# A sparse-graph network: the second layer's product 2 takes two of eight column blocks over edge lists, and list 0 is made in layer 0

## The chip, the cores and the metric

The kernel runs on one core of one Trainium2 chip. The core has a matrix engine (TensorE, PE in the profile), VectorE (DVE), ScalarE (ACT), GpSimd (POOL), and SyncE (SP), whose queue issues most loads; sixteen DMA engines are shared by all queues. Each engine works through its own instructions in the order that was fixed when the program was built. The metric is the device time of one execution in microseconds, smaller is better: the median of the runs.

## The reference

There are N = 4096 nodes with 128 features. The adjacency matrix `adj` is 4096 x 4096 in float32: about 0.2% of the entries are nonzero in symmetric places (each with a value of its own, from 0.05 to 1), and so is the diagonal. Four layers follow each other, each added to its input and normalized:

```
layer 0:  hw = x W;  e = leaky_relu of sums of hw over neighbours
          x <- norm(x + (softmax of e over a row's neighbours, times adj) hw)
layer 1:  twice cheb_conv(h) = h W[0] + (adj h) W[1] + (2 adj (adj h) - h) W[2] + b, then elu
layer 2:  attention of 4 heads over the columns of adj
layer 3:  x Ws + (adj x / row degree) Wn
```

The case is about layer 1 (the "second layer"). Its first convolution needs t1 = adj x (product 1) and adj t1 (product 2, for t2 = 2 adj t1 - x). The second one is arranged so that it takes two more products, of v (product 3) and of w (product 4).

## The kernel before

**Dense products.** `propagate` (L683) forms a product transposed, one block of 512 output columns at a time: for each of eight blocks `ib` it goes through eight chunks `c` of `adjT` (128 partitions x 4 x 512 floats, 1 MB each, loaded by SP's queue into a pool `ld` of five buffers, L661), with four matmuls of 128 x 512 each (L691), which the profile counts as two records each. So a product is 8 x 8 chunks. After each chunk a callback `seen(ib, n, c, a)` may add other work; a call of it is called a hook here. A block of `adj` columns is named by its number, 0 to 7; four tiles of 128 nodes make one.

**Edge lists.** Once the nonzeros of a block of four tiles are known, its product can be done by gathering the neighbours' rows instead: six near entries and three shared slots per node (`NEAR`, `QT`). The steps are
- `take` (L1319): for chunk (`ib`, `c`), the eight largest entries of each of four tiles' rows and their places, two VectorE instructions a tile (L1331, L1332). The list of block c needs all eight chunks (ib, c). On the diagonal chunk a copy by ACT (L1326) and three VectorE instructions (L1328 to L1330) take the own entry out and keep it in `diag`.
- `build` (L1340): three parts, each a `next`, that sort these into indices; small matmuls (L1382, L1406) stand between the parts.
- `pairs` (L1461) or `values` (L1455): gathers on Pool that fetch the entries' values, one indirect DMA for every 128 of them (L1452), each followed by a tiny "pause" (L1498). `pairs` gets both directions' values for the blocks in `PAIRED`; there are 4 x 9 gathers a block. `paired` (L1468) copies them to where they are used, in program order.
- `rows_of` (L1477): nine gathers that fetch one tile's neighbour rows from a table in DRAM, written by `store` (L1493) from ACT's queue. `weigh` (L1482): ACT scales the own row, three VectorE instructions make the slots' weights (L1486), and six add the near rows (L1489). Then PE multiplies, three or four matmuls of 128 x 128.

**Where they are used before the change.** Takes of even blocks run beside product 1, of odd blocks beside product 2. Beside product 2 the lists of blocks 0, 2 and 4 (`PAIRED`) are built and their 108 pairs gathered. Product 3 (`third_product`, L1528) does five blocks densely, and the twelve tiles of `PAIRED` over lists, beside building the other five lists. Product 4 (in `sparse_layers`, L1590) does six densely and the eight tiles of `LAST` = 0, 2 over lists. Layers 2 and 3 use all lists.

**Layer 0** (L281) works on the same chunks, row block by row block. For each chunk VectorE makes a mask (`masks`, L326), PE takes sums over the mask (L385), ACT looks for negative entries (L369), and PE multiplies (L397). From row block 2 on PE's order is written out by hand (`in_order`, L375): a group of mask sums, then that group's products. In block i >= 3 the first group is a chunk that was left over from the block before, then chunks 0 and 1, then another left-over one; then come product 0 and the scores of block i-1 (L427).

**Order.** Outside of parts that are written by hand, a planner orders each engine's instructions: program order decides among those that its model takes to be ready. `keep_in_program_order` pins an instruction behind the one traced before it on its engine.

**End of a block of product 2** (L740 to L754): VectorE makes t2T from the sum (L741), PE multiplies it and others by the first layer's weights (six matmuls of 128 x 512, L745), elu gives `hT`, and eight matmuls of 128 x 128 (L750) give v.

## Time and profile before

| | us |
|---|---|
| median of 3 runs | 1681.68 (1681.07 to 1682.41) |
| the profiled execution's own time | 1683.87 |
| its span (first to last instruction) | 1681.9 |
| layer 0, to the first matmul of product 1 | 0 to 329.8 |
| product 1 | 329.8 to 556.2 |
| product 2 | 556.2 to 846.9 |
| product 3 | 846.9 to 1048.7 |
| product 4, then layers 2 and 3 | 1048.7 to 1681.9 |

| engine | busy us | share of the span |
|---|---|---|
| PE | 1517.7 | 90% |
| DVE | 1089.2 | 65% |
| POOL | 749.3 | 45% |
| ACT | 372.4 | 22% |

A line of instructions gives the start, the length, the engine, the line of the kernel, the operation, the tiles written and read, and a count when several follow each other; in square brackets stands how long the engine stood idle before it and what ended that. A line of waits gives who waited for whom, then the sum, the times and the longest. Busy time is an average: what a change in one stage is worth is read from that stage.

### The profile page before, as it was taken

The numbers are of one execution on the slowest core, as the hardware profiler recorded it, in microseconds if no ns is written. First come the engines' busy times: TensorE is split into PE (matmuls) and PEld (weight loads), VectorE is DVE, ScalarE is ACT, GpSimd is POOL, SyncE is SP. The second block draws the span as 40 slices with busy tenths as digits, with TensorE's granted clock in tenths as the row PEclk, the third lists the DMA queues.
The fourth block names the chain that finished last, engine by engine and source line by source line (L and its number), as shares of the span: only waits on it lengthen the run. The fifth ranks groups of instructions, "written<-read, shape, count | busy, mean of one in ns | idle before, by whom it ended". The sixth has DMA issues, their size and how long they took to land.

```text
span 1681.9 us, 16311 instructions
## 1 busy us (share of the span) xinstructions
PE 1517.7 (90%) x4808; PEld 732.3 (44%) x4808; DVE 1089.2 (65%) x3189; ACT 372.4 (22%) x682; POOL 749.3 (45%) x1180
## 2 busy tenths in 40 slices
PE   6999999999999999999989899999955788889886
PEld 3344344544444444444434445454422344444444
DVE  5664546798779896888659832255434755557676
ACT  4865520100000011011110000022223111112234
POOL 0000000000000045555458888888827888888851
PEclk9999999999999999999989999999976888889988
DMA  9988756578888866777758868988846667778774
GB/s 383 355 314 304 254 200 225 194 288 311 299 298 298 311 209 218 255 247 243 258 203 280 311 224 286 336 296 283 296 108 182 212 199 232 238 235 277 240 198 105
DMA packets 102601, 429.24 MB, mean 255 GB/s; under 512 B 20387, under 2 KB 38822, under 8 KB 60646
## 3 DMA queue, kind: packets, MB, share of 16 engines
q1 hardware_dynamic: 62288, 376.79, 62.8%
q0 software_dynamic: 20352, 31.44, 7.4%
q10 hardware_dynamic: 19862, 19.86, 4.1%
q8 instruction: 40, 0.66, 0.2%
q14 instruction: 59, 0.48, 0.1%
HBM read 416.43 MB, written 11.60 MB: 254 GB/s over the span
## 4 chain that ended last, share of the span: by engine, by line
PE 59%; DVE 16%; DMA 9%; POOL 7%; issue 5%; ACT 2%; ACTq 0%; DVEq 0%; POOLq 0%; SPq 0%
PE pacc L691 24%; PE pacc L397 12%; PE pp L1918 8%; POOL got L1688 6%; DMA got<-table,source 4%; PE pp L1799 3%; DMA chunk<-in_adjT 3%; DVE at L1332 2%; DVE top L1331 2%; DVE gw L1724 1%; PE pden L385 1%; DMA got<-rows,source 1%; PE ptr L340 1%; DVE acc L1812 1%; DVE here L1726 1%
## 5 line engine op out<-in xcount | busy, mean ns | idle before, releaser
L1688 POOL DMA_INDIRECT got<-table,source x288 | 276.0, 958 | 88.6 <-issue 61.4
L1799 PE MATMUL pp<-chunk,xT 128*128 128x512 f32 x496 | 243.9, 633 | 1.2 <-ACT xT L1770 0.7
L691 PE MATMUL pacc<-chunk,t 128*128 128x512 f32 x512 | 223.8, 593 | 0.0
L691 PE MATMUL pacc<-chunk,x 128*128 128x512 f32 x512 | 222.0, 592 | 0.0
L1452 POOL DMA_INDIRECT got<-rows,source x180 | 180.9, 1005 | 60.2 <-issue 50.2
L397 PE MATMUL pacc<-chunk,hw 128*128 128x512 f32 x408 | 188.1, 605 | 1.5 <-DVE numT L425 1.2
L1331 DVE MAX8 top<-chunk 128x8 f32<-128x512 f32 x224 | 144.4, 677 | 55.4 <-DMA chunk<-in_adjT 55.4
L1918 PE MATMUL pp<-chunk,w 128*128 128x512 f32 x384 | 170.2, 592 | 0.0
L1498 POOL TENSOR_TENSOR idle<-v,idle 128x1 f32<-128x1 f32 x7 | 1.5, 211 | 336.5 <-ACT v L752 336.5
L1298 POOL IOTA i<- 128x384 int32 (+3 forms) x4 | 1.0, 260 | 337.1 <-PE pden L385 323.9
L1332 DVE FIND_INDEX8 at<-top,chunk 128x8 uint16<-128x512 f32 x224 | 151.1, 683 | 0.0
L691 PEld LDWEIGHTS pacc<-chunk,x 128*128 128x128 f32 x512 | 96.3, 190 | 116.2 <-issue 116.2
L691 PE MATMUL pacc<-chunk,v 128*128 128x512 f32 x320 | 145.3, 605 | 0.0
L691 PEld LDWEIGHTS pacc<-chunk,t 128*128 128x128 f32 x512 | 95.7, 190 | 113.4 <-issue 113.4
L1799 PEld LDWEIGHTS pp<-chunk,xT 128*128 128x128 f32 x496 | 94.3, 203 | 91.2 <-issue 84.6
L1452 POOL DMA_INDIRECT both_ways<-in_pairs,both_at x108 | 108.0, 1000 | 22.4 <-issue 17.8
L397 PEld LDWEIGHTS pacc<-chunk,hw 128*128 128x128 f32 x408 | 74.7, 191 | 92.7 <-issue 86.7
L328 DVE TENSOR_SCALAR pos<-chunk 128x2048 bf16<-128x2048 f32 x66 | 80.2, 1221 | 42.3 <-DMA chunk<-in_adjT 34.2
L1918 PEld LDWEIGHTS pp<-chunk,w 128*128 128x128 f32 x384 | 70.5, 190 | 76.5 <-issue 76.5
L369 ACT ACTIVATE junk<-chunk 128x2048 fp8e4<-128x2048 f32 x51 | 97.4, 1910 | 26.3 <-DMA chunk<-in_adjT 25.7
L1489 DVE SCALAR_TENSOR_TENSOR here<-got,back,here 128x128 f32<-128x128 f32 x120 | 42.0, 350 | 89.3 <-DMA got<-rows,source 86.3
L1498 POOL TENSOR_TENSOR idle<-idle 128x1 f32<-128x1 f32 x417 | 96.0, 230 | 7.4
(355 smaller groups left out, 1932.2 us busy)
## 6 DMA issues: line engine op xcount, KB each, us to landing
chunk<-in_adjT SPq DMA_DIRECT2D x342, 1024.0 KB, 5.3
keep<-in_adjT SPq DMA_DIRECT2D x13, 1024.0 KB, 10.6
spread<-spread ACTq DMA_DIRECT2D x16, 384.0 KB, 4.5
got<-table,source POOLq DMA_INDIRECT x288
chunk<-in_adjT ACTq DMA_DIRECT2D x4, 1024.0 KB
got<-rows,source POOLq DMA_INDIRECT x180
table<-rows ACTq DMA_DIRECT2D x8, 264.0 KB, 3.9
xT<-in_xT ACTq DMA_DIRECT2D x8, 256.0 KB, 6.6
```

What stands on the lines that cost most here:

```text
L328: r = nc.vector.tensor_scalar(pos, a, 0.0, None, op0=ALU.is_gt)
L369: nc.scalar.activation(junk, a, AF.Relu, scale=-1.0, accum_out=bad[:, n:n + 1], saturate=False)
L397: in_order(nc.tensor.matmul(p, hw[:, j * TB + k, :], a[:, k, :], start=first and k == 0, stop=last and k == TB - 1))
L691: nc.tensor.matmul(p, stationary(c * TB + k), a[:, k, :], start=n == 0 and k == 0, stop=n == NB - 1 and k == TB - 1)
L1331: nc.vector.max(self.top[:, t, ib, :], row)
L1332: nc.vector.max_index(self.at[:, t, ib, :], self.top[:, t, ib, :], row)
L1452: tc.keep_in_program_order(nc.gpsimd.indirect_dma_start(out, None, of, bass.IndirectOffsetOnAxis(ap=index, axis=0)))
L1489: r = nc.vector.scalar_tensor_tensor(here, got[:, j, 0:F], self.back[:, u, j:j + 1], here, op0=ALU.mult, op1=ALU.add)
L1498: return nc.gpsimd.tensor_tensor(self.idle[:, 0:1], of, self.idle[:, 1:2], ALU.mult)
L1688: nc.gpsimd.indirect_dma_start(got[t][:, j, :], None, table, bass.IndirectOffsetOnAxis(ap=lists.source[:, t, j:j + 1], axis=0))
L1799: nc.tensor.matmul(p, y[:, t0 + k, :], a[:, ib % (TB // n), k, :], start=k == 0, stop=k == n - 1)
L1918: nc.tensor.matmul(p, w[:, c * TB + k, :], a[:, k, :], start=n == 0 and k == 0, stop=n == NB - 1 and k == TB - 1)
```

## The change

`PAIRED` becomes 0, 1, 2 and `LAST` 0, 1. In product 2 only blocks 2 to 7 are dense; blocks 0 and 1 go over lists. For that

- the takes of column block 0 move into layer 0 (`first_list`), to the chunk j = 0 of each row block. The host lays the diagonal of `adj` out as an input, so that one instruction takes it off in place of three;
- product 1 takes its blocks in the order 2, 3, 0, 4, 5, 1, 6, 7, with takes of columns 1 to 3, and of 4 to 7 in blocks 0 and 1. List 0 is built beside its second and third block, its 36 pairs are gathered beside the later ones, and t1 is stored as a third table of rows;
- product 2 takes columns 4 to 7 of its six blocks, pinned, and a written plan (`second_product`) says at which of its 48 hooks lists 1 and 2 are built, pairs and rows gathered, and the eight tiles weighed and multiplied. Rows are gathered into parts of `hT`, `t1T` and `xT` that aren't used yet or any more. The end of a block is now a function, called for the list blocks too;
- product 3 builds lists 3 to 7, and its plan is one hook later.

The diff, without its unchanged lines ("..." stands for them):

```diff
-PAIRED = [0, 2, 4]
-LAST = [0, 2]
+PAIRED = [0, 1, 2]
+LAST = [0, 1]
+FAR = [4, 5, 6, 7]
...
-def adj_resnorm_d4(ctx: ExitStack, tc: tile.TileContext, x_in, xT_in, adj, adjT, pairs, w0g, w0gT, a0, w1a, b1a,
+def adj_resnorm_d4(ctx: ExitStack, tc: tile.TileContext, x_in, xT_in, adj, adjT, pairs, diag_in, w0g, w0gT, a0, w1a, b1a,
...
+            def first_list(i, a):
+                top, at = firsts
+                for k in range(TB):
+                    row = a[:, k, :]
+                    if i == 0:
+                        row = x[:, k * TB:(k + 1) * TB, :].rearrange("p t f -> p (t f)")
+                        nc.scalar.copy(row, a[:, k, :])
+                        d = row[:, k * P:(k + 1) * P]
+                        nc.vector.scalar_tensor_tensor(d, ident, less_own[0][:, k:k + 1], d, op0=ALU.mult, op1=ALU.add)
+                    nc.vector.max(top[:, k, i, :], row)
+                    nc.vector.max_index(at[:, k, i, :], top[:, k, i, :], row)
...
+                    if j == 0:
+                        first_list(i, a)
...
+                if j == 0:
+                    first_list(i, a)
...
-    degrees = []
+    degrees, firsts, less_own = [], [], []
...
-                    degrees[:] = [enter(name="degrees", bufs=1).tile([P, NT], F32, name="rowdeg")]
+                    early = enter(name="early", bufs=1)
+                    degrees[:] = [early.tile([P, NT], F32, name="rowdeg")]
+                    firsts[:] = early.tile([P, TB, NB, 8], F32, name="top0"), early.tile([P, TB, NB, 8], U16, name="at0")
+                    own_entries = early.tile([P, NT], F32, name="diag")
+                    less_own[:] = [early.tile([P, NT], F32, name="less_own")]
+                    nc.scalar.dma_start(own_entries, diag_in)
+                    nc.vector.tensor_scalar_mul(less_own[0], own_entries, -1.0)
...
-                    lists = Lists(whole, first, l1h_pool)
+                    lists = Lists(whole, first, l1h_pool, own_entries)
...
-                for ib, blk, p in propagate(lambda jt: x[:, jt, :], finished, seen=lambda ib, n, c, a: c % 2 or lists.take(ib, c, a)):
+                pairs = {c: lists.pairs(c) for c in PAIRED} if usual else {}
+                def fetch(c, n):
+                    for _ in range(n):
+                        next(pairs[c], None)
+                made = lists.build(0) if usual else None
+                done = []
+                def beside_first(ib, n, c, a):
+                    if 0 < c < FAR[0] or ib in LAST and c in FAR:
+                        lists.take(ib, c, a)
+                    if (len(done), n) in ((1, 0), (1, 4), (2, 0)):
+                        next(made)
+                    if len(done) > 2 and n == 3:
+                        tc.keep_in_program_order(lists.pause(t1[:, done[-1] * TB, 0:1]))
+                        fetch(0, TB * 9 // 4)
+                for ib, blk, p in propagate(lambda jt: x[:, jt, :], finished, seen=beside_first, blocks=[2, 3, 0, 4, 5, 1, 6, 7]):
...
+                    done.append(ib)
+                    if usual:
+                        lists.store(2, ib, t1)
...
-                steps, pairs = {}, deque()
-                def fetch(n):
-                    while pairs and n:
-                        if next(pairs[0], pairs) is pairs:
-                            pairs.popleft()
-                        else:
-                            n -= 1
-                for n, c in enumerate(PAIRED if usual else ()):
-                    made = lists.build(c)
-                    steps[2 * n, 0], steps[2 * n, 4] = [lambda made=made: next(made)], [lambda made=made: next(made)]
-                    steps[2 * n + 1, 0] = [lambda made=made: next(made), lambda c=c: pairs.append(lists.pairs(c))]
-                def second(ib, n, c, a):
-                    if c % 2:
-                        lists.take(ib, c, a)
-                    for f in steps.pop((ib, n), ()):
-                        f()
-                    if usual and ib and n == 3:
-                        tc.keep_in_program_order(lists.pause(v[:, ib * TB - 1, 0:1]))
-                        fetch(16)
-                for ib, blk, p in propagate(lambda jt: t1[:, jt, :], seen=lambda ib, n, c, a: second(ib, n, c, a)):
-                    t2T = l1w.tile([P, IB], F32, name="t2T")
-                    nc.vector.scalar_tensor_tensor(t2T, p, 2.0, xT[:, blk], op0=ALU.mult, op1=ALU.subtract)
+                def t2_of(t2T, p, cols):
+                    nc.vector.scalar_tensor_tensor(t2T, p, 2.0, xT[:, cols], op0=ALU.mult, op1=ALU.subtract)
+                def second_end(ib, t2T):
+                    blk = slice(ib * IB, (ib + 1) * IB)
...
+                    done[-1] = ib
...
+                second = second_product(lists, l1w, pairs, t1, t1T, xT, hT, v, done, t2_of, second_end) if usual else None
+                for ib, blk, p in propagate(lambda jt: t1[:, jt, :], seen=second, blocks=[b for b in range(NB) if not usual or b not in LAST]):
+                    t2T = l1w.tile([P, IB], F32, name="t2T")
+                    t2_of(t2T, p, blk)
+                    second_end(ib, t2T)
...
-                    fetch(len(pairs) * TB * 9)
-                    for c in PAIRED:
-                        lists.paired(c)
+                    fetch(PAIRED[-1], TB * 9)
+                    lists.paired(PAIRED[-1])
...
-        def __init__(self, whole, first, layer):
+        def __init__(self, whole, first, layer, own_entries):
...
-            self.tables = [dram.tile([N + 1, F], F32, name=f"rows{n}") for n in range(2)]
+            self.tables = [dram.tile([N + 1, F], F32, name=f"rows{n}") for n in range(3)]
...
-            self.at = keep.tile([P, NT, NB, 8], U16, name="at")
-            self.diag = keep.tile([P, NT], F32, name="diag")
+            self.at = keep.tile([P, NT - TB, NB, 8], U16, name="at")
+            self.diag = own_entries
...
-        def take(self, ib, c, a):
+        def take(self, ib, c, a, pinned=False):
+            pin = tc.keep_in_program_order if pinned else lambda r: r
...
-                    own = self.keep.tile([P, P], F32, name="diagonal")
...
-                    nc.vector.tensor_mul(own, d, ident)
-                    nc.vector.tensor_reduce(self.diag[:, t:t + 1], own, AX.X, ALU.add)
-                    nc.vector.tensor_sub(d, d, own)
-                nc.vector.max(self.top[:, t, ib, :], row)
-                nc.vector.max_index(self.at[:, t, ib, :], self.top[:, t, ib, :], row)
+                    pin(nc.vector.scalar_tensor_tensor(d, ident, less_own[0][:, t:t + 1], d, op0=ALU.mult, op1=ALU.add))
+                pin(nc.vector.max(self.top[:, t, ib, :], row))
+                pin(nc.vector.max_index(self.at[:, t - TB, ib, :], self.top[:, t, ib, :], row))
...
-            top = self.top[:, ts]
+            top, found_at = (self.top[:, ts], self.at[:, (c - 1) * TB:c * TB]) if c else firsts
...
-            nc.vector.tensor_copy(flat(key), flat(self.at[:, ts]))
+            nc.vector.tensor_copy(flat(key), flat(found_at))
...
+    def second_product(lists, pool, pairs, t1, t1T, xT, hT, v, done, t2_of, second_end):
+        units = len(LAST) * TB
+        E = NEAR + QT
+        late = slice(5 * IB, 8 * IB)
+        soon = slice(2 * IB, 5 * IB)
+        places = [t[:, cols].rearrange("p (j f) -> p j f", f=F)
+                  for t, cols in ((hT[:, 0], late), (hT[:, 1], late), (t1T, soon), (xT, soon))]
+        got = places[0:2] + places[2:4] * (units // 2 - 1)
+        made, sums = {}, {}
+        plan = {}
+        def at(h, f, *args):
+            plan.setdefault(h, []).append(lambda: f(*args))
+        def fetch(c, n):
+            for _ in range(n):
+                next(pairs[c], None)
+        def pull(u):
+            deque(lists.rows_of(u, got[u], 2), 0)
+        def weigh(u):
+            here = pool.tile([P, F], F32, name="here2", bufs=1)
+            lists.weigh(u, t1[:, tile_of(u), :], got[u], here, got[u][:, E:E + QT, :], True)
+            made[u] = here
+        def product(u):
+            t, k = tile_of(u), u % TB
+            if k == 0:
+                sums[0] = pool.tile([P, IB], F32, name="t2T")
+            p = lists.psum.tile([P, P], F32, name="u")
+            nc.tensor.matmul(p, made.pop(u), ident, start=True, stop=False)
+            for j in range(QT):
+                nc.tensor.matmul(p, got[u][:, j, :], got[u][:, E + j, :], start=False, stop=j == QT - 1)
+            t2_of(sums[0][:, k * P:(k + 1) * P], p, slice(t * P, (t + 1) * P))
+            if k == TB - 1:
+                second_end(PAIRED[u // TB], sums.pop(0))
+        for c, h in ((1, 0), (2, 8)):
+            build = lists.build(c)
+            for n in range(3):
+                at(h + 3 * n, next, build)
+        at(6, fetch, 1, TB * E)
+        at(11, pull, 0)
+        at(12, pull, 1)
+        at(17, fetch, 2, 9)
+        at(18, lists.paired, 0)
+        at(30, lists.paired, 1)
+        for u, h in enumerate((20, 24, 28, 32, 33, 37, 40, 41)):
+            at(h, weigh, u)
+            at(h + 1, product, u)
+        for u, h in ((2, 25), (3, 25), (4, 29), (5, 33), (6, 34), (7, 38)):
+            at(h, pull, u)
+        at(40, fetch, 2, TB * E)
+        hooks = [0]
+        def seen(ib, n, c, a):
+            h = hooks[0]
+            hooks[0] += 1
+            if c in FAR:
+                lists.take(ib, c, a, True)
+            for f in plan.pop(h, ()):
+                f()
+            if h == 47:
+                assert not plan and not made and not sums
+        return seen
...
-            for c in (6, 1, 3, 5, 7):
+            for c in (3, 4, 5, 6, 7):
...
-        plan = {5: [lambda: deque(lists.values(6), 0)]}
-        for u, h in enumerate((6, 8, 14, 17, 19, 22, 24, 27, 30, 32, 35, 37)):
+        plan = {5: [lambda: deque(lists.values(3), 0)]}
+        for u, h in enumerate((7, 9, 15, 18, 20, 23, 25, 28, 31, 33, 36, 38)):
...
-        plan[36].append(lambda: deque(lists.values(1), 0))
+        plan[36].append(lambda: deque(lists.values(4), 0))
...
-                for c in (3, 5, 7):
+                for c in (5, 6, 7):
...
-            order = [0, 1, 2, 3, 5, 6, 4, 7]
+            order = [0, 1, 3, 4, 5, 6, 2, 7]
...
+        "diag": column_blocks(np.diagonal(adj)),
```

## The prediction

> **What bounds the kernel now.** I read the chain of waits first, then busy time stage by stage, then single instructions. Of the chain that ended last, these lines carry it:
>
> ```profile
> PE 59%; DVE 16%; DMA 9%; POOL 7%; issue 5%; ACT 2%; ACTq 0%; DVEq 0%; POOLq 0%; SPq 0%
> ```
>
> TensorE's matmuls are most of it. Cut into stages (columns: stretch, its length, then busy us and instructions of each engine, granted clock, DMA share, GB/s): layer 0's DMA-heavy start, the rest of layer 0, product 1, product 2, product 3.
>
> ```profile
> 0.00:81.50 81.50, 64.27 (x315) 29.30 (x316) 48.38 (x114) 51.86 (x56) 0.69 (x6) 0.94 0.94 374
> 81.50:329.80 248.30, 245.69 (x927) 110.90 (x926) 140.24 (x333) 95.15 (x114) 0.81 (x5) 1.00 0.70 251
> 329.80:556.20 226.40, 225.79 (x566) 101.81 (x565) 196.20 (x545) 16.13 (x28) 0.59 (x3) 1.00 0.82 295
> 556.20:846.90 290.70, 278.39 (x764) 127.77 (x763) 230.50 (x687) 43.43 (x73) 133.44 (x223) 1.00 0.72 247
> ```
>
> From 81.5 us through product 2 PE is busy nearly all the time; VectorE (third busy figure) is at 57%, 87% and 79% of the last three stretches, and Pool only works in product 2. So a matmul removed from product 2 is time removed, unless VectorE or Pool is made late. Product 2 takes 290.7/8 = 36.3 us per column block. The prices, from the timelines of PE, VectorE and Pool (start, length, what):
>
> ```profile
> 816.34 25.06 PE L691 MATMUL pacc<-chunk,t 128*128 128x512 f32 x58
> ...
> 1079.57 0.39 PE L1894 MATMUL pp<-ident,here 128*128 128x128 f32 x2
> 1079.79 0.83 PE L1896 MATMUL pp<-into,got 128*128 128x128 f32 x6
> 1080.46 3.60 PE L1918 MATMUL pp<-chunk,w 128*128 128x512 f32 x8
> ```
>
> ```profile
> 601.64 1.27 DVE L1331 MAX8 top<-chunk 128x8 f32<-128x512 f32 x2
> ...
> 604.15 0.27 DVE L1354 TENSOR_SCALAR there<-top 128x256 f32<-128x256 f32 x1
> ```
>
> ```profile
> 601.99 1.17 POOL L1452 DMA_INDIRECT both_ways<-in_pairs,both_at  x1 [4.05 <-DVE both_at L1434]
> 603.20 0.20 POOL L1498 TENSOR_TENSOR idle<-idle 128x1 f32<-128x1 f32 x1
> 603.55 0.99 POOL L1452 DMA_INDIRECT both_ways<-in_pairs,both_at  x1 [0.15 <-issue]
> 604.55 0.21 POOL L1498 TENSOR_TENSOR idle<-idle 128x1 f32<-128x1 f32 x1
> 604.92 0.97 POOL L1452 DMA_INDIRECT both_ways<-in_pairs,both_at  x1 [0.15 <-issue]
> ```
>
> 58 of a block's 64 records run from 816.34 to 841.24 (start of the next), 0.43 us each: a dense block is 27.5 us, a chunk 3.44 us. One tile's product over lists is 1080.46 - 1079.57 = 0.89 us. Two tiles of a take (maxima and their places) last from 601.64 to 604.15, so a chunk of four is 5.02 us. Gathers follow each other every 604.92 - 603.55 = 1.37 us (1.36 further on).
>
> Last, where a late gather hits PE today, at the start of product 3:
>
> ```profile
> 868.73 0.35 DVE L1489 SCALAR_TENSOR_TENSOR here<-got,back,here 128x128 f32<-128x128 f32 x1 [7.54 <-DMA got<-rows,source]
> ...
> 876.40 0.16 PE L1382 MATMUL u<-count,below 128*128 128x4 bf16 x1 [8.02 <-DVE count L1358]
> 876.43 6.74 PE L691 MATMUL pacc<-chunk,v 128*128 128x512 f32 x8
> ```
>
> The row read at 868.73 was asked for by the fourth gather, which left Pool at 864.13: 4.6 us to land. VectorE stood at it, the counts behind it came late, PE waited 8.02 us, and its next eight records took 6.74 us instead of the 3.60 of line L1918 above.
>
> **What the Trainium skill says.** Perfetto Trace Analysis, Sequencer Loop: an engine instruction goes into the engine's queue and waits there for its semaphores. The trace agrees: one late row held all of VectorE for 7.54 us. DMA: Bandwidth & Descriptors, Anatomy of one DMA (SWDGE path): about 2.0 us fixed cost, mostly the receipt of the write; the trace shows 4.6 us beside the chunk loads, and I use that. TensorE: Matmul & The Clock Gate, HAM oscillation: PE gaps over about 3.4 us drop its clock; the 6.74 us above agree, so a long stall costs some 3.1 us on top.
>
> **The change part by part.** The sums are against the profiled execution: span 1681.9 us, its own time 1683.9, median of the runs 1681.7; a difference carries over to the median.
>
> *Removed:* two dense blocks of product 2, 2 x 27.5 = 55.0 us of PE, and 16 chunk loads with them (no price: DMA is at 0.72). *Added on PE:* eight products of 0.89 = 7.1 us. The two blocks' ends (hidden layer, v) stay. With nothing late: -47.9.
>
> *Moved: takes of column block 0 into layer 0.* Eight chunks x 5.02 = 40.2, and four diagonal fixes of 0.35 (as L1489, same operands' size): 41.6 us of VectorE, in bursts of 5.0 right behind a chunk's mask and ahead of the next chunk's mask and of the scores. PE there must have the masks in order, and today waits only 4.0 us for them. Block by block: in the start, VectorE has some 7.5 us idle between 38 and 58 us, and gets 6.4 + 5.0 = 11.4: about 4 late, and 1 more with what scores waits for. Block 2's masks are back to back from 68 to 75 and PE wants the last at 76.6: 3.5 late. Block 3: last mask at 107.4, PE at 108.9, 2 us of idle before: 1.8 late. Block 4: the chunks land at 127.5, 130.5 and 134.8, gaps that hold the burst: 0. Block 5: they land 2.5 us apart, burst 2.5 late. Blocks 6 and 7: landings 4 to 6.9 apart: 0. Sum 12.8, less something for the waits it overlaps (1.15 us at 171.4 is one): I take 12. Bounds: 0 (idle takes all) to 41.6.
>
> *Product 1.* Takes are 24 chunks plus 8 extra ones of blocks 0 and 1: 32 as before. But those blocks have seven takes, 35.1 us of VectorE in 28.3 of PE, and list 0 is built around block 0 (some 15 us by its rows from 604 to 608 and 575 to 601). Cover: the takes may lead PE by about 8 us (five chunk buffers, 5.3 us landing) and lag it by 8. Nothing taken; 0 to 6 us if that cover is short. The three-instruction diagonal becomes one: VectorE slack only. The 36 pair gathers run on an idle Pool; eight t1 stores on ACT's queue (256 KB; a like one lands in 3.9 us) are wanted 60 us later; 16 KB of diagonal at the start: nothing.
>
> *Product 2's timing.* Places count from its start. List 1's third part is issued at hook 6, PE 7 x 3.44 = 24.1 us; in the old trace 8.8 us passed from that matmul (593.2) to the first gather (602.0), so Pool starts at 32.9. It has 36 pairs and 9 rows ahead of the first weigh: 45 x 1.36 = 61.2, plus 4.6 landing: 98.7. That weigh is at hook 20, its product behind chunk 21: 2 x 36.3 + 6 x 3.44 = 93.2. PE waits 5.5. Queued on VectorE behind it are three pinned takes, 15.1 us, until 114, and then that block's t2T; PE gets there at 98.7 + 0.9 + 6.9 + 1.7 = 108.2 and waits about 6 more. With 3.1 of lost clock: 14.6. The next rows: tile 2's places are free after block 4 (about 116), Pool idle then; rows at 133 against hook 28 at about 134. Later ones have 5 us or more to spare. Pool ends its 144 gathers at about 249 of some 258, so product 3's start keeps its own stall. I take 15; bounds 0 (VectorE's order lets block 4's end pass) to 25 (the first take of the block is stuck behind the rows too, another 5, and a second tile waits once).
>
> *Product 3 and 4:* five lists to build, 12 and 8 tiles, the same gathers; each weigh one hook later, other column numbers. Zero, give or take 5.
>
> Sum: -47.9 + 12 + 15 = -20.9: 1681.7 - 20.9 = 1660.8, say 1661.
>
> **The rivals.** *Covered everywhere* (chance 0.25): VectorE's 43% idle in layer 0 takes the bursts and the order on VectorE is one that the late row does not block; -47.9 plus 3 to 5: 1637. For it: idle share; against: the masks' leads of 1 to 4 us against bursts of 5. *Gathers slower* (0.13): beside full DMA the pace is nearer 1.5 us (product 3's lines show 1.35 to 2.0). Then the first rows are 45 x 0.14 = 6 later, and a second tile waits, some 5: 1672. Pool is then nearly the bound of the stage: 144 x 1.5 + 33 = 249 plus landing. *Slower than before* (0.12): layer 0's bursts are on PE's path in full. Place: masks and scores of each row block; price 41.6; with the 15 of product 2 that is -47.9 + 56.6 = +8.7, 1690. It decides from 32.9 of the 41.6 on. Against: three blocks have landing gaps that hold a burst. That the change doesn't act, the dense blocks being skipped by name, can't be; the general path would only follow a failed list check, and would take many times the difference. About even (1678 to 1685, gathers and layer 0 both near their bad ends): 0.05.
>
> **How the numbers follow.** Forecast 1661 (chance 0.45, its own range 1649 to 1671). Its lower neighbour at 1637 plus or minus 7 and the slower cases above give 1635 to 1683 for eight in ten: it leaves out a third of the covered case, and most of the slower one. Faster than 1678.3, which is 0.2% (about what a measurement can tell): 0.45 + 0.25 + 0.12 + 0.03 = 0.85; within 0.2%: 0.03; slower: 0.12.
>
> **What would show it.** Product 2 some 33 us shorter, 512 records of L691 with t down to 384; one VectorE wait on got<-rows of over 10 us about 85 us into product 2 and PE's t2T wait at the end of its third dense block; layer 0 ending 8 to 16 us later, with PE's waits for pos up from 4.0; no change in product 1. Layer 0 unmoved, or no wait at the first weigh, makes me too high; PE waiting in product 1, or at every weigh, too low.

## The result, and the profile after

| | before | after |
|---|---|---|
| median, us (22 runs each, measured together) | 1681.3 (1677.7 to 1687.8) | 1675.1 (1669.2 to 1682.2) |
| the profiled execution's own time | 1683.9 | 1672.2 |
| its span | 1681.9 | 1670.4 |

The ratio is 0.9956 (95% interval 0.9944 to 0.9967): about 7.4 us faster (the two medians differ by 6.2). The forecast was 20.9 us faster, 1661. The spans of the two profiled executions differ by 11.5 us; 5.6 us of that is their place among the runs (the one before lies 2.6 us above its median, the one after 3.0 below).

By stage, from the first matmul of each, in us:

| stage | before | after | difference | forecast |
|---|---|---|---|---|
| layer 0 | 329.8 | 350.9 | +21.1 | +12 |
| product 1 | 226.4 | 226.3 | -0.1 | 0 |
| product 2 | 290.7 | 256.3 | -34.4 | -55.0 + 7.1 + 15 = -32.9 |
| product 3 | 201.8 | 203.1 | +1.3 | 0 |
| product 4 and on | 633.2 | 633.8 | +0.6 | 0 |

The stretches of the profile after that answer to those of before (length, busy us and instructions of each engine, granted clock, DMA share, GB/s): start of layer 0, the rest of it, product 1, product 2.

```profile
0.00:81.50 81.50, 55.05 (x269) 26.85 (x270) 51.93 (x137) 44.84 (x50) 0.68 (x6) 0.87 0.84 321
81.50:350.90 269.40, 262.12 (x972) 117.33 (x971) 176.41 (x409) 104.25 (x125) 0.81 (x5) 0.98 0.67 246
350.90:577.20 226.30, 226.30 (x580) 102.04 (x579) 197.53 (x577) 14.18 (x25) 44.02 (x80) 1.00 0.85 307
577.20:833.50 256.30, 232.42 (x687) 111.23 (x686) 194.13 (x567) 43.28 (x75) 175.99 (x288) 0.97 0.67 228
```

In the first 81.5 us TensorE does 55.05 us of work instead of 64.27, at a clock of 0.87 instead of 0.94. Over all of layer 0 VectorE has 228.3 busy us instead of 188.6: 39.7 more, where the forecast had 41.6. Of TensorE's waits within layer 0 (sum, times, longest), the first line is from before, where it waited for pos (a mask); the other three are from after:

```profile
PE pden L385 <- DVE pos L328: 4.0, 3, 1.6
...
PE pden L398 <- DVE pos L329: 9.0, 7, 2.9
PE ptr L405 <- DVE parts L445: 4.6, 1, 4.6
PE pmm L358 <- DVE hw L360: 3.5, 1, 3.5
```

Where each comes from is in the timelines of TensorE and VectorE for the start:

```profile
21.64 0.18 DVE L680 TENSOR_SCALAR less_own<-diag 128x32 f32<-128x32 f32 x1 [3.52 <-DMA diag<-in_diag]
22.37 2.83 PE L358 MATMUL pmm<-WA,xT 128*128 128x132 f32 x12 [3.46 <-DVE hw L360]
...
42.41 0.35 DVE L376 SCALAR_TENSOR_TENSOR x<-ident,less_own,x 128x128 f32<-128x128 f32 x1
42.79 0.69 DVE L377 MAX8 top<-x 128x8 f32<-128x512 f32 x1
...
47.36 0.68 DVE L377 MAX8 top<-x 128x8 f32<-128x512 f32 x1
47.95 0.67 DVE L445 COPY parts<-pden 128x512 f32<-128x512 f32 x1
...
48.68 1.87 PE L405 MATMUL ptr<-sel,parts 128*128 128x3 f32 x8 [4.59 <-DVE parts L445]
```

Two things are to be seen. The multiplication of the diagonal by -1, which nothing needs before 42 us, stands early in VectorE's order and waits 3.52 us for its 16 KB; the copies of the projected features (hw, L360) are queued behind it, and TensorE's projections behind those. And the list of block 0, from 42.41 on, stands ahead of the copy of the sums (parts) that TensorE waits for: the copy ends at 48.6, and TensorE stood idle for 4.59 us.

Product 2 on VectorE and TensorE:

```profile
666.61 0.35 DVE L1517 SCALAR_TENSOR_TENSOR here<-hT,back,here 128x128 f32<-128x128 f32 x1 [14.30 <-DMA hT<-rows,source]
...
671.95 0.49 PE L1587 MATMUL u<-ident,here 128*128 128x128 f32 x2 [1.13 <-DVE here L1517]
...
698.29 2.07 PE L769 MATMUL pmm<-t2T,W1A 128*128 128x512 f32 x2 [16.59 <-DVE t2T L762]
```

The first weigh holds VectorE for 14.30 us, until 89 us into the product. TensorE hardly notices at the list product itself (1.13), but what is queued on VectorE behind the weigh (takes, and the sorting of list 2) makes t2T late at the end of the third dense block, 121 us in: 16.59 us.

For what follows: in five of the six later groups of runs the kernel before itself took 1765 to 1785 us, not 1680, a condition that isn't fixed to one chip (the same chip showed 1766 in one group and 1680 in another), so a kernel's total is compared only inside its group.

### The profile page after: what moved, and what is told of

Its sections match the earlier page's. It is cut to its first block, busy times and chain, and to the rows that moved or that the text cites. A ratio compares the mean times of both kernels' runs of the same rounds, so it can differ in the third digit from the quotient of the medians.

```text
span 1670.4 us, 16412 instructions
## 1 busy us (share of the span) xinstructions
PE 1480.9 (89%) x4744; PEld 719.1 (43%) x4744; DVE 1096.5 (66%) x3204; ACT 374.8 (22%) x690; POOL 835.3 (50%) x1322
## 4 chain that ended last, share of the span: by engine, by line
PE 50%; DVE 20%; POOL 12%; DMA 9%; issue 6%; ACT 3%; SPq 1%; ACTq 0%; DVEq 0%; POOLq 0%
PE pacc L714 19%; PE pacc L410 11%; PE pp L2013 7%; POOL got L1783 5%; DMA got<-table,source 5%; DVE at L1360 3%; POOL got L1480 3%; DVE top L1359 2%; PE pp L1894 2%; POOL both_ways L1480 2%; DMA got<-rows,source 2%; POOL idle L1526 2%; DVE gw L1819 2%; DVE acc L1907 2%; DMA chunk<-in_adjT 1%
## 5 line engine op out<-in xcount | busy, mean ns | idle before, releaser
L410 PE MATMUL pacc<-chunk,hw 128*128 128x512 f32 x408 | 192.1, 616 | 0.2
L714 PE MATMUL pacc<-chunk,t 128*128 128x512 f32 x384 | 170.0, 593 | 0.0
L1359 DVE MAX8 top<-chunk 128x8 f32<-128x512 f32 x196 | 128.4, 677 | 17.6 <-DMA chunk<-in_adjT 17.6
L1360 DVE FIND_INDEX8 at<-top,chunk 128x8 uint16<-128x512 f32 x196 | 133.0, 684 | 0.0
L1526 POOL TENSOR_TENSOR idle<-idle 128x1 f32<-128x1 f32 x489 | 111.2, 227 | 8.5
L1517 DVE SCALAR_TENSOR_TENSOR here<-got,back,here 128x128 f32<-128x128 f32 x120 | 42.2, 351 | 100.9 <-DMA got<-rows,source 98.7
L714 PEld LDWEIGHTS pacc<-chunk,t 128*128 128x128 f32 x384 | 71.1, 190 | 81.0 <-issue 81.0
L382 ACT ACTIVATE junk<-chunk 128x2048 fp8e4<-128x2048 f32 x51 | 97.4, 1910 | 32.9 <-DMA chunk<-in_adjT 32.2
L714 PEld LDWEIGHTS pacc<-chunk,v 128*128 128x128 f32 x320 | 60.5, 194 | 78.2 <-issue 78.2
```

The costliest lines, as they stand in the source:

```text
L382: nc.scalar.activation(junk, a, AF.Relu, scale=-1.0, accum_out=bad[:, n:n + 1], saturate=False)
L410: in_order(nc.tensor.matmul(p, hw[:, j * TB + k, :], a[:, k, :], start=first and k == 0, stop=last and k == TB - 1))
L714: nc.tensor.matmul(p, stationary(c * TB + k), a[:, k, :], start=n == 0 and k == 0, stop=n == NB - 1 and k == TB - 1)
L1359: pin(nc.vector.max(self.top[:, t, ib, :], row))
L1360: pin(nc.vector.max_index(self.at[:, t - TB, ib, :], self.top[:, t, ib, :], row))
L1517: r = nc.vector.scalar_tensor_tensor(here, got[:, j, 0:F], self.back[:, u, j:j + 1], here, op0=ALU.mult, op1=ALU.add)
```

## The experiments

Layer 0 and product 1 last the same in all groups of runs (product 1 226 us in every profile; layer 0 of the changed kernel 349.1 to 351.6), so they can be read against the first profiles.

Stage lengths of the profiles used below, in us (layer 0; products 2, 3, 4; all behind them), and the ratio to the kernel before of the same group:

| run | layer 0 | 2 | 3 | 4 | behind | ratio (interval) |
|---|---|---|---|---|---|---|
| first measurement, before | 329.8 | 290.7 | 201.8 | 231.2 | 402.0 | 1 |
| first measurement, after | 350.9 | 256.3 | 203.1 | 229.6 | 404.2 | 0.9956 |
| x1_negate_on_gpsimd | 345.6 | 313.0 | 236.9 | 245.3 | 469.2 | 1.032 (1.027 to 1.037) |
| x2_rows_ahead | 349.1 | 287.0 | 241.0 | 246.1 | 469.9 | 1.028 (1.023 to 1.032) |
| x3_no_first_list | 332.0 | 302.4 | 233.6 | 273.8 | 474.8 | 1.046 (1.042 to 1.049) |
| x4_list_later | 341.0 | 308.1 | 235.3 | 240.8 | 475.6 | 1.034 (1.030 to 1.038) |
| y1_before_again | 328.4 | 288.9 | 213.1 | 248.9 | 459.2 | 1.002 (0.999 to 1.004) |
| y2_after_again | 351.6 | 298.2 | 227.0 | 238.7 | 463.5 | 1.030 (1.025 to 1.036) |
| y3_negate_and_rows | 346.1 | 269.2 | 231.0 | 238.4 | 465.9 | 1.015 (1.011 to 1.019) |
| y4_with_list_later | 337.9 | 275.2 | 235.2 | 239.7 | 467.5 | 1.013 (1.008 to 1.018) |
| z0_after_third | 349.1 | 297.9 | 239.7 | 238.4 | 471.0 | 1.033 (1.028 to 1.037) |
| z1_rows_ahead_again | 350.3 | 297.8 | 243.4 | 230.5 | 466.7 | 1.012 (1.007 to 1.017) |
| z2_three_edits_again | 339.1 | 291.4 | 233.9 | 234.7 | 465.3 | 1.011 (1.007 to 1.015) |
| w0_after_fourth | 351.5 | 313.3 | 242.3 | 234.2 | 471.3 | 1.035 (1.028 to 1.042) |
| w1_dense_product_2 | 350.9 | 306.3 | 217.9 | 255.9 | 474.2 | 1.026 (1.020 to 1.033) |
| w2_gathers_spaced | 351.0 | 280.4 | 237.6 | 251.7 | 474.6 | 1.017 (1.010 to 1.023) |
| v1_four_edits | 339.7 | 256.2 | 235.8 | 254.1 | 403.7 | 1.021 (1.019 to 1.023) |
| v2_before_spaced | 328.4 | 285.5 | 231.8 | 255.3 | 401.2 | 1.030 (1.028 to 1.032) |
| u1_rows_ahead_third | 351.5 | 295.8 | 245.3 | 248.1 | 474.0 | 1.019 (1.014 to 1.025) |
| u2_three_edits_third | 334.5 | 293.4 | 241.9 | 241.2 | 471.1 | 1.019 (1.013 to 1.024) |

The stage lengths are those of one profiled execution, the ratio is that of the runs of the group. The profiled executions of z1 and u1 lie 24 and 20 us above the medians of their kernels, so their stages behind product 1 can't be compared closely.

**Layer 0.** The theory: the 21.1 us are the wait for the diagonal and the bursts of the list, both by their place in VectorE's order. The rivals: the start is bound by loads anyway, or VectorE's sum of work, not its order, is what counts. Three kernels, each the changed one with one edit.

```diff
-nc.vector.tensor_scalar_mul(less_own[0], own_entries, -1.0)
+nc.gpsimd.tensor_scalar_mul(less_own[0], own_entries, -1.0)
```

> Against the changed kernel one instruction moves: the multiplication of the loaded diagonal by -1 goes from VectorE to GpSimd, so that VectorE no longer stands 3.5 us for the diagonal's load at 18 us into the span. Theory A (the 4.5 us that the matmuls of the start came late, and that stayed to the end of layer 0, are this wait): first matmul of block 0's column sums at about 44.2 us instead of 48.7, layer 0 ends 4 to 5 us earlier (346 instead of 350.9), total 4 to 5 us less than the changed kernel. Theory B (the start is bound elsewhere, by the loads of the features or of the first chunks, and the wait only takes the place of another): layer 0 ends within 1.5 us of 350.9.

Layer 0 ended at 345.6, 5.3 us earlier, with the column sums of block 0 at 44.67 instead of 48.68. The wait for hw is gone from TensorE's list. Theory A for layer 0; the rival falls. (The changed kernel itself was not run in this group, so the forecast for the total isn't tested.)

x3 leaves out the list of layer 0. Its values and places are set to zero once, on GpSimd, so that all later parts work with an empty list 0:

```diff
+nc.gpsimd.memset(firsts[0]..., 0.0)
+nc.gpsimd.memset(firsts[1]..., 0)
...
 def first_list(i, a):
+    return
...
+nc.vector.tensor_scalar(flag, flag, 0, None, op0=ALU.mult)
```

> Left out against the changed kernel: all of the work on list 0 in layer 0 (32 pairs of maximum and index, the four copies and the four diagonal corrections of block 0). The list's values and indices are set to zero once, so everything after layer 0 issues the same instructions on an empty list 0, whose row gathers all fetch few addresses. The flag of the fallback is held at zero. The diagonal's load and its multiplication by -1 stay. Theory A (the bursts on VectorE cost layer 0 16 to 17 us, and the wait for the diagonal the other 4.5): layer 0 ends at 333 to 336 us instead of 350.9 and the total is 15 to 17 us less. Theory B (the prediction's size of 12 us, the rest being the state of the memory or the clock): layer 0 ends at 338 to 342. Theory C (the bursts are hidden and something else of the change slows layer 0): layer 0 ends within 4 us of 350.9.

Layer 0 ended at 332.0, just below the 333 to 336 of theory A: the bursts cost 18.9 us, a little more than the 16 to 17 expected. Of VectorE's 39.7 us that is just under half. What remains against the kernel before is 2.2 us; at block 0's column sums it is 4.1 (43.87 against 39.80), the diagonal's wait, of which later row blocks give back 1.9. The two edits' gains, 5.3 and 18.9, are more than the 21.1 there is, so they overlap by 3. The total of this kernel says nothing on the change: its empty list sends every row gather of list 0 to few addresses, and the packets of GpSimd's queue, as many packets and bytes as before, took 15.6% of the DMA engines' time instead of 7.7 (third part of the page, of x1 first, then of x3):

```profile
q0 software_dynamic: 22656, 36.17, 7.7%
```

```profile
q0 software_dynamic: 22656, 36.17, 15.6%
```

x4 keeps the work and emits it one group of chunks later (one of the places of the edit; the others are alike):

```diff
+if later:
+    first_list(*later.pop())
 if j == 0:
-    first_list(i, a)
+    later.append((i, a))
```

> Against the changed kernel the same instructions of list 0 in layer 0 are emitted one group of chunks later in each row block (for block 0 behind the copy of the sums, for block 1 behind the next chunk's mask, for the others behind the second or the following group's masks), so that VectorE makes the masks and the copy of the sums first. Theory A (the cost of 16 to 17 us comes from the bursts standing ahead of masks and of the copy that TensorE waits for at once): layer 0 ends 8 to 14 us earlier than 350.9, TensorE's waits for pos and parts fall under 2 us each. Theory B (the cost is VectorE's load: about 40 us more of busy time in a stage where VectorE has to make every mask): wherever the burst stands it costs the same, layer 0 ends within 4 us of 350.9.

Layer 0 ended at 341.0, 9.9 us earlier. TensorE's wait for parts is gone and that for pos is back at 4.1 us, as before the change (under 2 was expected). So about half of the bursts' price is order, and VectorE's load alone doesn't set it. The other 9 us stay: 341.0 against 332.0; by the column sums 6.3 of them arise in row blocks 0 and 1.

**Product 2, and what the later groups added.** x2 moves the row transfers of tiles 0 and 1 ahead of list 1's pairs:

```diff
+at(0, pull, 0)
+at(1, pull, 1)
 at(6, fetch, 1, TB * E)
-at(11, pull, 0)
-at(12, pull, 1)
```

> Against the changed kernel the row transfers of tiles 0 and 1 of the first product block stand ahead of list 1's 36 pair gathers in GpSimd's order, instead of behind them. Nothing else is changed. Theory A (the 16.6 us that TensorE stands for t2T at the end of the third dense block, with VectorE standing 14.3 us for got, are the lateness of the first rows): both waits fall under 4 us, product 2 is 13 to 18 us shorter (about 240 us instead of 256.5), total 13 to 18 us less than the changed kernel. Theory B (GpSimd's queue is the bound of product 2: what is pulled ahead delays list 1, whose rows come 3 us later each, and the same wait appears at a later tile): product 2 within 5 us of 256.5, with a VectorE wait for rows of 10 us or more at a later place.

Product 2 took 287.0 us, where the changed kernel's profile had 256.3 and x1 and x4 of the same group 313.0 and 308.1. In all four kernels of the group the chain of waits had an entry of its own for releasers that the profile can't name, and the longest in product 2 of x1 was this, on VectorE:

```profile
674.44 0.17 DVE L1442 TENSOR_TENSOR nth<-place,u 128x12 f32<-128x12 f32 x1 [38.83 <-remote]
```

Its operand u was made by TensorE at 632. In the first two profiles no such wait exists. One caution: the profiles of the five groups in this condition hold 11.5 to 13.3 thousand records of semaphores (the signals between engines and queues; w2 below has 16.1), those of the first measurement and of v1 and v2 21.5 to 23.2. An unnamed releaser can therefore be one whose record is missing, and whether the recording has a part in the condition is not tested. The next group therefore took both kernels unchanged, with two sums of edits.

> The kernel before, unchanged, for its profile on the chip of this group of runs. In the group before this one the kernel before took 1778.7 us instead of 1681.7, and the variants of the changed kernel lost in product 2, 3 and 4 what they had won in layer 0: 214 to 239 us of waits there that end on a releaser which the profile can't name. Theory A (these waits belong to the chip, and the gathers on GpSimd's queue meet them): on a chip with 1779 us this profile shows such waits too, but fewer than the changed kernel's; on a chip with 1681 us it shows none. Theory B (they come from the edits of those variants): this profile shows none on either chip.

> The changed kernel, unchanged, beside the kernel before on the same chip. Theory A (the unnamed waits belong to the chip): where the kernel before takes 1779 us this takes 1835 to 1855 us (4 to 10 us more than the variants with an edit), with layer 0 ending at 351 us as on the first chip, and the sign of the change turns with the chip; where the kernel before takes 1681 us this takes 1672 to 1678. Theory B (the edits): this is faster than the kernel before by 0.2 to 0.7% on either chip.

> The changed kernel with two edits: the multiplication of the diagonal on GpSimd, and the row transfers of tiles 0 and 1 ahead of list 1's pair gathers. On a chip where the kernel before takes 1681 us, theory A (the wait for the diagonal and the late first rows are two separate losses that add up): 17 to 23 us less than the changed kernel in the same group (5.3 us of it in layer 0, 13 to 18 in product 2). Theory B (the rows' wait only moves on to the next tile): 4 to 8 us less. On a chip where the kernel before takes 1779 us, by the runs so far, 15 to 25 us less.

> The two edits and the list of layer 0 emitted one group of chunks later, together. Theory A (three separate losses of layer 0 and product 2): layer 0 ends at 334 to 338 us, and the total is 26 to 33 us less than the changed kernel's in the same group, so about 1645 us where the kernel before takes 1681. Theory B (the later list only moves the load of VectorE to the start of product 1): layer 0 ends at about 336 us, and product 1 is 5 us or more longer than 226.

The kernel before took 1771 us and has such waits too, though none in product 2; y2 has them in product 2 as well; so it isn't the edits. The changed kernel, untouched, was 3.0% slower than it: in this condition the sign of the change turns. Layer 0 costs 23 us here, much as in the first measurement; product 2 takes 298.2, 9 more than the kernel before's 288.9 instead of 34 less; product 3 14 more. The two edits gave 29 us (1820.2 to 1791.3). The third gave another 5, which is less than the spread of the runs (1779 to 1799 for both kernels). Layer 0 fell to 337.9, inside the 334 to 338 that was expected; y3's 346.1 against y2's 351.6 repeats what x1 showed.

> The changed kernel, unchanged, as the measure for the two beside it. In the two groups before, the kernel before took 1779 and 1766 us and the changed kernel was 3% slower than it, by product 2 (292 and more instead of 256.5 us). Theory A (that is a matter of the chip, or of what else runs on it): where the kernel before takes 1676 to 1688 us here, this takes 1669 to 1682 and product 2 is 256 to 258 us; where it takes 1750 us or more, this is again 2.5 to 3.5% slower. Theory B (the first measurement was the exception): 3% slower whatever the kernel before takes.

> The changed kernel with the row transfers of tiles 0 and 1 ahead of list 1's pair gathers, alone. Where the kernel before takes 1676 to 1688 us: theory A (late first rows are the whole of the 16.6 us wait) product 2 is 239 to 243 us and the total 13 to 18 us less than the changed kernel beside it; theory B (GpSimd's order only moves the wait) product 2 is 252 us or more. Where the kernel before takes 1750 us or more: product 2 shorter than the changed kernel's by 15 to 30 us, as in the first two groups.

> The three edits together. Where the kernel before takes 1676 to 1688 us: layer 0 ends at 336 to 339 us, product 2 takes 239 to 243, and the total is 26 to 33 us less than the changed kernel's beside it, 1643 to 1649 us, so faster than the kernel before by about 2%; if the losses are not separate (the rival), 1655 us or more. Where the kernel before takes 1750 us or more: 30 to 38 us less than the changed kernel, 1.0 to 1.5% slower than the kernel before.

The kernel before took 1765 us; the changed kernel 1821.3 (1.033, 1.028 to 1.037), rows ahead 1792.7 (1.012, 1.007 to 1.017), three edits 1787.7 (1.011, 1.007 to 1.015). This is theory A of z0, and rows ahead is worth 29 us here. That is more than the wait it was made for, so it doesn't prove the wait's size. Nor do the profiles show where it comes from: product 2 of z1's takes 297.8 us, like z0's 297.9, where 15 to 30 us less were expected (z1's execution lies 24 us above its median), and z2's 291.4.

Next, one part undone and one suspect slowed: w1 makes product 2 dense again, without the row gathers; w2 puts two pauses behind each gather.

```diff
-for ib, blk, p in propagate(..., seen=second, blocks=[b for b in range(NB) if not usual or b not in LAST]):
+for ib, blk, p in propagate(..., seen=second):
...
-at(11, pull, 0)
-at(12, pull, 1)
...
-for u, h in enumerate((20, 24, 28, 32, 33, 37, 40, 41)):
-    at(h, weigh, u)
-    at(h + 1, product, u)
-for u, h in ((2, 25), (3, 25), (4, 29), (5, 33), (6, 34), (7, 38)):
-    at(h, pull, u)
```

```diff
 tc.keep_in_program_order(nc.gpsimd.indirect_dma_start(...))
 tc.keep_in_program_order(self.pause())
+tc.keep_in_program_order(self.pause())
```

> The changed kernel, unchanged, as the measure for the two beside it. Where the kernel before takes 1750 us or more, 1.030 to 1.033 of it, as in the two groups before; where it takes 1676 to 1688 us, 1669 to 1682 us, with product 2 at 256 to 258 us.

> One part of the change undone: product 2 takes all eight column blocks densely again, so its 72 row gathers, their 72 weighted sums and the eight list products are gone; the lists themselves are still made where the change makes them, with the diagonal's load and the list of layer 0. Where the kernel before takes 1676 to 1688 us: product 2 takes 288 to 293 us, and the total is 33 to 36 us more than the changed kernel. Where the kernel before takes 1750 us or more: theory A (the 72 row gathers of product 2 are what loses there) product 2 takes 289 to 293 us like the kernel before's, not more than the changed kernel's 292, product 3 falls from 227 to about 213 us, and the total is equal to the changed kernel's or below it by up to 20 us, 1.02 to 1.03 of the kernel before; theory B (the loss there lies in the other parts) the total is 20 us or more above the changed kernel's.

> The changed kernel with two pauses of GpSimd instead of one behind each of the 420 gathers of products 1 to 4, so that one gather takes about 1.71 us of its order instead of 1.36. Where the kernel before takes 1676 to 1688 us: list 1's 36 gathers and the 18 of the first rows take 19 us more, and TensorE waits that much longer for them in product 2, total 10 to 25 us more than the changed kernel. Where the kernel before takes 1750 us or more: theory A (gathers that follow each other too closely stall the other engines) product 2 takes 260 to 280 us instead of 292, total 10 us or more less; theory B (the spacing is not the cause) total 10 to 30 us more.

w1: 1833.7 against the changed kernel's 1844.3; so the total fits theory A, but product 2 took 306.3, not 289 to 293, and product 3 217.9 instead of 213. The list products are worth nothing in this condition, and yet most of the loss is there without the 72 row gathers: 50.8 of 61.4 us. w2 was the surprise: slower gathers (1.61 us apart instead of 1.35) made the kernel 26.7 us faster, 1817.7. Product 2 of each as a stretch, w0 first, then w2:

```profile
577.80:891.10 313.30, 239.40 (x688) 112.86 (x687) 193.62 (x567) 43.61 (x75) 175.91 (x288) 0.89 0.55 188
```

```profile
577.30:857.70 280.40, 238.73 (x688) 115.05 (x687) 194.70 (x567) 43.30 (x75) 199.83 (x416) 0.93 0.62 209
```

The work of the other engines is the same; GpSimd is 24 us busier, and yet the stage is 33 us shorter. What happens in w0 is seen on three engines at once:

```profile
645.46 0.59 PE L714 MATMUL pacc<-chunk,t 128*128 128x512 f32 x1 [0.84 <-issue]
645.94 0.97 POOL L1480 DMA_INDIRECT both_ways<-in_pairs,both_at  x1 [0.15 <-issue]
646.86 0.59 PE L714 MATMUL pacc<-chunk,t 128*128 128x512 f32 x1 [0.81 <-issue]
647.29 0.97 POOL L1480 DMA_INDIRECT both_ways<-in_pairs,both_at  x1 [0.15 <-issue]
...
682.38 0.97 POOL L1480 DMA_INDIRECT hT<-rows,source  x1 [0.15 <-issue]
...
687.01 0.17 DVE L1442 TENSOR_TENSOR nth<-place,u 128x12 f32<-128x12 f32 x1 [43.08 <-remote]
```

From 642.6 to 654.7 us TensorE, which waits for nothing that the profile shows, does only one matmul every 1.4 us, about the pace of the gathers, and VectorE's wait ends 4.6 us after the last gather of the stream starts. (In x1 the last gather of the stream starts at 674.02, and the wait ends at 674.44.) In w2's product 2 no wait ends on an unnamed releaser; in the 14 profiles of the changed kernel and its variants with the closer gathers, in this condition, such waits sum to 27 to 124 us there. They don't always fall on nth: in y2 and z0, the same kernel as w0, nth waits only 5.9 and 7.1 us, and ScalarE carries most of the sum. In w2 TensorE keeps its usual pace where w0 stood (42 records in 18.19 us from 652.37 on). So it is shown that the spacing shortens the kernel in this condition, and nth's wait and TensorE's slow stretch are gone in w2; other waits may only have got a name, since its profile holds more records. That closely spaced gathers stall the other engines is what fits; by which path isn't shown, and w2 is still 1.7% slower than the kernel before.

The last two groups took all four edits together, the spacing alone, and the edits without the spacing.

> The changed kernel with the negation on GpSimd, the row transfers of tiles 0 and 1 ahead, the list of layer 0 later, and two pauses behind each gather. Where the kernel before takes 1750 us or more: the three edits gave 34 us and the spacing 27 us; theory A (they are separate) 50 to 60 us less than the changed kernel, so 0.995 to 1.005 of the kernel before; theory B (both mend the same waits of product 2) 30 to 40 us less, 1.010 to 1.015 of it. Layer 0 ends at 337 to 340 us. Where the kernel before takes 1676 to 1688 us: 1648 to 1662.

> The kernel before with two pauses behind each of its 348 gathers of products 2 to 4. Where the kernel before takes 1750 us or more: theory A (close gathers stall the engines in every kernel, and the change only has more of them at a time) 10 us or more faster than the kernel before, by products 3 and 4; theory B (the loss needs the change's rows in product 2) within 5 us of it or slower. Where the kernel before takes 1676 to 1688 us: 0 to 15 us more, by later rows in product 3.

This group fell into the condition of the first measurement: the kernel before took 1680.2 us. v1 missed its forecast by far: 1715.8 us instead of 1648 to 1662. Layer 0 ended at 339.7, inside the 337 to 340; but products 3 and 4 took 33 and 25 us more than in the changed kernel as first measured. The spacing alone costs the kernel before 50.7 us (1730.9), 30 in product 3 and 24 in product 4, much more than the 0 to 15 expected: VectorE's waits for rows, the kernel before as first measured and then v2:

```profile
DVE here L1489 <- DMA got<-rows,source: 86.3, 32, 12.1
```

```profile
DVE here L1490 <- DMA got<-rows,source: 158.3, 59, 23.1
```

Both kernels of the group have that spacing, so their difference is the change with its three other edits: 1715.8 against 1730.9, 15.2 us faster. Layer 0 is 11.3 us longer, product 2 29.3 shorter. In v1 the wait at hT is gone, and TensorE's wait at the third dense block's end is 0.99 us instead of 16.59. But with gathers that are a fifth slower the rows of tile 2 come late, and TensorE waits 7.92 us at the end of the fourth dense block (1.18 in the changed kernel):

```profile
669.68 1.12 PE L779 MATMUL pmm<-t2T,W1A 128*128 128x512 f32 x2 [0.99 <-DVE t2T L772]
...
689.42 0.35 DVE L1528 SCALAR_TENSOR_TENSOR here<-t1T,back,here 128x128 f32<-128x128 f32 x1 [10.77 <-DMA t1T<-rows,source]
...
716.89 2.08 PE L779 MATMUL pmm<-t2T,W1A 128*128 128x512 f32 x2 [7.92 <-DVE t2T L772]
```

So the late first rows were the cause of the wait at the third block's end: of v1's other edits two end with layer 0, and the spacing only slows the rows. Product 2 as a whole is no shorter for it here (256.2 us against 256.3), as theory B of x2 had it, but with the slower gathers.

> The changed kernel with the row transfers of tiles 0 and 1 ahead of list 1's pair gathers, alone. Where the kernel before takes 1676 to 1688 us: theory A (late first rows are the whole of the 16.6 us wait) product 2 takes 239 to 243 us and the total is 0.985 to 0.989 of the kernel before (the changed kernel: 0.9956); theory B (GpSimd's order only moves the wait) product 2 takes 252 us or more, and 0.993 or more of the kernel before. Where the kernel before takes 1750 us or more: 1.010 to 1.028, as before.

> The three edits together, gathers not spaced. Where the kernel before takes 1676 to 1688 us: layer 0 ends at 336 to 339 us, product 2 takes 239 to 243, total 0.977 to 0.981 of the kernel before; if the losses are not separate 0.985 or more. Where the kernel before takes 1750 us or more: 1.010 to 1.015, as before.

The kernel before took 1785 us again: rows ahead 1823.2 (1.019, 1.014 to 1.025), three edits 1813.4 (1.019, 1.013 to 1.024, above the 1.010 to 1.015 expected), layer 0 of it at 334.5. How much time rows ahead gains where the kernel before takes 1680 and the gathers aren't spaced, and whether the three edits without the spacing beat both kernels there, stays open. No kernel run was faster than the kernel before in its own group, except the changed kernel in the first measurement.

## Why the prediction was wrong

The two steps that failed both lie in layer 0: the diagonal's load, put at nothing, cost 5.3 us, and the bursts of the takes, put at 12, cost 18.9.

**16 KB of diagonal: nothing.** Wrong, 5.3 us (x1). The load was priced by its bytes. What counted was the instruction that needs it, ahead of the copies of the projected features in VectorE's order, and eight feature loads ahead of it on ACT's queue.

**Bursts of layer 0: +12.** This is the larger miss: 18.9 us (x3). The start of each row block's column sums, in us, shows where it arises:

| row block | 0 | 1 | 2 | 3 | 4 | 5 | 6 | 7 |
|---|---|---|---|---|---|---|---|---|
| x3, without the list | 43.87 | 62.83 | 88.40 | 117.27 | 145.82 | 179.13 | 214.95 | 255.08 |
| after | 48.68 | 72.08 | 98.29 | 131.64 | 160.33 | 198.01 | 233.83 | 273.96 |
| lost in this block | 4.8 | 4.4 | 0.6 | 4.5 | 0.1 | 4.4 | 0 | 0 |
| forecast | 5, with block 1 | | 3.5 | 1.8 | 0 | 2.5 | 0 | 0 |

Blocks 4, 6 and 7, with gaps between their chunks, hold their bursts, as forecast. In blocks 0 and 1, 9.2 us of the bursts' 11.4 show, where 5 were forecast: the arithmetic set the bursts against VectorE's idle time near by, but in block 0 the burst stands ahead of the copy that TensorE wants. In blocks 3 and 5 the lateness itself was about right: TensorE waits 2.4 us more for masks in block 3 than in x3 (1.8 forecast), and 2.5 more in block 5 (2.5). What the forecast left out there is the slower work behind the wait, which it had priced only for the long stall of product 2: the first records behind the wait take some 1.7 us more in each of the two blocks. For block 3, after and then x3, where the granted clock was 0.81 and 1.00:

```profile
101.17 8.81 PE L410 MATMUL pacc<-chunk,hw 128*128 128x512 f32 x16
```

```profile
89.83 7.13 PE L414 MATMUL pacc<-chunk,hw 128*128 128x512 f32 x16
```

The wait ahead of the 8.81 us was 1.27 us long, among small matmuls. The bounds, 0 to 41.6, held the 18.9.

The other terms:

- *Dense blocks removed, list products added (-47.9), and the stall of product 2 (+15).* The size was right: together -34.4 against -32.9, so the stall was 13.5. The profiles agree: TensorE's waits in product 2 rose from 12.0 to 23.6 us, and the first records behind the long one took 1.9 us more than usual. The mechanism was half right. A late first row, a wait of VectorE and a late t2T came as described, but nearly all of the stall stood at t2T (16.6) and not 5.5 us at the first list product and 6 at t2T. The rows came sooner: the first gather left 30.0 us into the product, not 32.9, and the last of tile 0's rows was used 94.3 us in, not 98.7. Between there and t2T VectorE then did, by the starts in its timeline, 16.9 us of takes (15.1 forecast) and 7.4 us of list 2's sorting, which the forecast didn't have there. That these differences nearly cancel is luck. That the late rows set this wait is shown by v1.
- *Product 1: 0.* Right, in every profile. Products 3 and 4: +1.3 and, with all behind, +0.6. Right.
- *Sum.* 21.1 - 0.1 - 34.4 + 1.3 + 0.6 = -11.5 of the profiled spans; layer 0's 9 us are nearly the whole miss against -20.9. The medians moved by 6.2 only: the two profiled executions flattered the change by 5 us, and no stage of theirs shows where these went.
- *The rivals.* "Covered everywhere" fell with layer 0 and with the wait at t2T. "Gathers slower", 1672, comes close to the measured time by luck: in product 2 the gathers left every 1.35 us, with a few longer steps 1.40 on average over the first 81, not every 1.5. "Slower than before" wanted layer 0's bursts in full, 32.9 of 41.6; they reached 18.9. In the later groups the changed kernel was slower, by 3.0 to 3.5%, in a condition that the first profile didn't show and that no rival named. The pace of the gathers is part of it (26.7 of 61.4 us came back in w2); the rest stays open.

## What to carry to other kernels

Work that is moved to an idle engine is paid where it stands in that engine's order, not by the engine's idle share: price it against the instruction behind it that another engine waits for, add what the other engine loses in pace behind the wait, and give a small load's first user a late place or another engine. Follow each new instruction that waits for a DMA, even one of 16 KB. And a gain of half a per cent that rests on many small gathers wants measuring more than once: here the same two kernels stood at 0.996 in one measurement and at 1.030 to 1.035 in three others.

## What the hardware showed that was not expected

- In one condition of the machine two pauses instead of one behind each gather (1.61 us apart instead of 1.35) made the changed kernel 26.7 us faster; in the other the same spacing made the kernel before 50.7 us slower.
- In the first of these conditions one VectorE instruction of 0.17 us waited 38.8 us (x1) and 43.1 us (w0) with its TensorE operand long done, until 0.4 and 4.6 us after the last gather of a stream started; for some of that time TensorE did only one matmul every 1.4 us.
- Gathers of the same size and number took twice the DMA time (15.6% against 7.7) when those of one list all fetched few addresses.
- A wait of TensorE of only 1.27 us, among small matmuls, was followed by a granted clock of 0.81 and 1.7 us of slower work (layer 0, row block 3).
